# The attention's opening, and the gates of the second routing, of a macaron block rearranged

## Chip, cores and metric

One core of a Trainium2 chip runs the whole program. The metric is the device time of one execution in microseconds (us). A PE matmul's speed follows a clock that the profile gives as "granted clock", 1.00 being full speed.

## What is computed

An input x of 8 sequences x 1024 tokens x 512 features in f32, 8192 tokens in all, goes through three residual steps. The reference in short:

```python
x = x + 0.5 * moe(layernorm(x))
x = x + attention(layernorm(x))      # 16 heads of 32, rotary q and k, softmax(q k / sqrt(32)) v, then Wo
x = x + 0.5 * moe(layernorm(x))

def moe(h):                          # 32 experts, the same weights both times
    probs = softmax(h @ w_router)                    # one expert per token, the best
    top1 = argmax(probs); gate = probs[top1]
    pos = cumsum(onehot(top1)) - 1                   # the token's place in its expert, in order of tokens
    accepted = pos < 320                             # 1.25 * 8192 / 32
    y = (silu(buf @ w_gate) * (buf @ w_up)) @ w_down # buf: each expert's tokens
    return h + where(accepted, gate * y, 0)
```

## The kernel before

The program has six parts, one after the other. Times are those of the profiled execution.

- **First routing** (`front`, 0 to 114): all tokens are normalized and routed; it ends with the tables `come` (which token each of an expert's 3 blocks of up to 128 rows takes) and `go` (where its result goes).
- **First branch** (114 to 119): the program chooses one of four lists of expert widths by the counts. Each engine jumps by itself.
- **First experts** (`experts`, 119 to 877): for each of 32 experts POOL gathers rows by token, PE transposes, multiplies by the three weights, and POOL scatters the result. `fetch_gates` (L883) gathers each token's gate by token beside them; it runs only in this stage, from the tensor `gates`.
- **Attention** (`Attention`, 877 to 3571), in 32 units (sequence b, four heads c).
- **Second branch**, at 3571, and **second experts** (3575 to 4337), the same code with other sources.

Inside the attention PE, ACT, DVE and POOL do their instructions in the order in which the program records them; SP, which starts most transfers, has an order chosen by a scheduler.

*Opening* (L1569). The eight x tiles of the first sequence are fetched on SP in two halves of four; for each tile DVE takes the statistics (`measure`, L164 to L180), POOL the square root (L176), ACT normalizes (L185), PE transposes (L207), and ACT and DVE in turn copy into `hT` (L1619). On the second tile half k and q of the next positions can be made. `project` (L1661) makes q and k groups: eight matmuls (L1221), a bias, a turn for the rotary part (L1709) and its arithmetic, and copies of 32 rows into `swapped` and `cross` (L1732), which the scores read. The opening does k0 and q0 of the first 512 positions, then k1; q1 is left to the first stage.

*Stage* (`stage`, L1252). A stage has 16 slots and lays two things into each: the "top" scores of one unit (L1842, whose maximum DVE takes at L1850 and whose exponential and sum ACT takes at L1854; only the maximum and the sum are kept) and the weighted sums of the unit before (L1813, L1820, L1822, L1910). PE's free time in a slot is filled by `fill` (L1373): groups of q and k of the following unit, of values (`values`, L1753, 16 matmuls of L1240), or of the output. A group may lie in one slot or in pieces in several. The first stage has no unit before, so only top scores and groups: twelve whole groups in slots 0 to 11 and none in slots 12 to 15:

```python
v, self.v_groups = self.v_groups[:7], self.v_groups[7:]
return dict(zip((0, 2, 4, 6, 8), ahead + qk)) | dict(zip((1, 3, 5, 7, 9, 10, 11), v))
```

`joined` (L1466, begun in slot 0) multiplies the router into Wo (L1482) and afterwards the biases of v and o into rows (L1494, L1506). `prepare` (L1534) normalizes the next sequence during a stage.

*Second routing* (`finished`, L2048, `route`, L238). As soon as four tiles of the attention's output are done, their routing follows: maximum of the logits, place in the expert (a scan), the slot number, the square root of the variance (`scaled`), the exponentials and the gate. Then (L303) POOL scatters, for each of the four tiles, one pair (token, gate) a row into `table` (L307), 64 scatters in 16 routings. In the last routing the four scatters carry the token alone, ahead of the gate, and the gates go to a second table `late` by `Late.put` (L745) inside the second experts.

*Behind the second branch* (`places`, L765): SP reads the table (L778), DVE folds its last block, PE transposes it (L788), DVE makes `come` (L790) and `go`; after the first expert's up-projections the `late` table is read, added, and transposed as the gates.

## Time and profile before

| quantity | value |
|---|---|
| runs | 4362.11, 4370.67, 4372.54; median 4370.67 us |
| profiled execution | 4346.86 us, of it the span 4345.1 us |
| granted clock, mean | 0.987 |
| first unit's top scores to its last | 917.5 to 1003.0 us |
| units after it | about 78.6 us each |
| first gather of the second experts | 3577.11 us |
| scatters into the table | 60 land in 2.6 us, the late 4 in 6.6 us (medians) |

PE is TensorE's matmuls, PEld its weight loads, DVE VectorE, ACT ScalarE, POOL GpSimd, SP the engine that issues most transfers. In a line of instructions, the first number is the start in us, the second the duration; "x4" is a group of four; in brackets stands the idle time of the engine just ahead and what ended it. In a table of stretches, each engine has its busy time and number of instructions.

### The profile page before, as it was taken

To read this page: it belongs to the slowest core of one execution; us is meant where nothing else is said; L and a number is where in the kernel's file an instruction comes from. 1 tells how busy PE (TensorE), PEld (TensorE's weight loads), DVE (VectorE), ACT (ScalarE), POOL (GpSimd) and SP (SyncE) were. 2 spreads that over 40 slices of the span, in tenths; PEclk is the share of its full clock that TensorE was granted. 3 is DMA by queue.
4 is the path that set the end of the run, shared out by engine and by line. 5 is a ranking of instruction groups with operands and counts; after the bars stand their busy time and mean duration, and the time that the engine had idled before them with its cause. 6 is when DMAs were issued, how large, how long until landed. Compare 5 with 4: busy or idle time off the path is not lost.

```text
span 4345.1 us, 84352 instructions
## 1 busy us (share of the span) xinstructions
PE 4233.0 (97%) x32310; PEld 2407.5 (55%) x32310; DVE 2600.6 (60%) x4964; ACT 2616.9 (60%) x4325; POOL 1401.0 (32%) x1640
## 2 busy tenths in 40 slices
PE   8899999979999999999999999999999979999999
PEld 6566777844444444444444444444444436667777
DVE  8434433356766776876876776776866754344333
ACT  6112221237888888888888888888888842112121
POOL 7344444421222242242232232232232213333332
PEclk9999999989999999999999999999999989999999
DMA  4656666531112212212212212212212116566664
GB/s 157 217 185 204 206 204 229 197 111 48 50 42 71 79 46 65 80 48 65 77 48 65 79 47 65 81 47 63 80 42 60 38 59 206 191 202 202 217 228 162
DMA packets 310835, 495.59 MB, mean 114 GB/s; under 512 B 65049, under 2 KB 99235, under 8 KB 310418
## 3 DMA queue, kind: packets, MB, share of 16 engines
q1 hardware_dynamic: 269698, 412.06, 31.0%
q0 software_dynamic: 39776, 76.77, 5.5%
q8 instruction: 257, 4.21, 0.4%
q14 instruction: 160, 1.31, 0.1%
q10 hardware_dynamic: 944, 1.23, 0.1%
HBM read 379.85 MB, written 87.93 MB: 108 GB/s over the span
## 4 chain that ended last, share of the span: by engine, by line
PE 91%; DVE 3%; issue 2%; ACT 1%; POOL 1%; DMA 1%; POOLq 0%; ACTq 0%; SPq 0%; DVEq 0%
PE s L1240 11%; PE s L1842 11%; PE s L1221 11%; PE gp L969 10%; PE up L969 10%; PE s L1910 10%; PE s L1813 10%; PE yp L1015 9%; PE s L1806 4%; PE tp L957 2%; PE yp L1023 1%; DVE nm L1850 1%; ACT s L1854 1%; PE s L207 1%; DVE st L164 1%
## 5 line engine op out<-in xcount | busy, mean ns | idle before, releaser
L1850 DVE TENSOR_REDUCE nm<-s 128x1 f32<-128x1024 f32 x1024 | 1205.6, 1219 | 541.7 <-PE s L1842 540.3
L1854 ACT ACTIVATE s<-s,nm 128x1024 f32<-128x1024 f32 x1024 | 1114.3, 1088 | 149.9 <-DVE nm L1850 141.3
L974 ACT ACTIVATE sg<-gp 128x320 f32<-128x320 f32 (+7 forms) x256 | 99.5, 389 | 1061.8 <-PE gp L969 1060.8
L1820 ACT ACTIVATE pr<-s 128x512 f32<-128x512 f32 x992 | 538.1, 594 | 230.7 <-PE s L1813 226.8
L1748 POOL TENSOR_TENSOR raw<-raw,a 128x512 f32<-128x512 f32 x125 | 158.6, 1269 | 1312.6 <-DMA rot<-raw 957.3
L1842 PE MATMUL s<-cross,swapped 32*128 32x512 f32 x2048 | 560.4, 607 | 5.4 <-DMA cross<-k 3.1
L1842 PE MATMUL s<-k,q 32*128 32x512 f32 x2048 | 560.1, 603 | 0.0
L1822 ACT ACTIVATE pr<-s 128x1024 f32<-128x1024 f32 x528 | 542.9, 1031 | 19.7 <-PE s L1813 19.7
L1813 PE MATMUL s<-q,k 32*128 32x512 f32 x4096 | 538.4, 590 | 0.0
L1221 PE MATMUL s<-hT,wqk 128*32 128x128 f32 (+3 forms) x4720 | 503.3, 324 | 8.8 <-ACT pr L1820 4.9
L1910 PE MATMUL s<-pr,big 128*32 128x512 f32 x4096 | 492.7, 598 | 0.5 <-ACT pr L1822 0.5
L969 PE MATMUL gp<-bT,wg 128*128 128x272 f32 (+7 forms) x1984 | 488.7, 389 | 0.0
L969 PE MATMUL up<-bT,wu 128*128 128x272 f32 (+7 forms) x1984 | 484.9, 387 | 0.0
L1221 PEld LDWEIGHTS s<-hT,wqk 128*32 128x32 f32 (+1 forms) x4720 | 299.1, 129 | 286.1 <-ACT pr L1820 101.6
L1015 PE MATMUL yp<-wd,a 128*128 128x512 f32 x992 | 445.9, 592 | 0.0
L969 PEld LDWEIGHTS gp<-bT,wg 128*128 128x128 f32 x1984 | 371.6, 190 | 87.4 <-issue 21.4
L969 PEld LDWEIGHTS up<-bT,wu 128*128 128x128 f32 x1984 | 374.4, 190 | 70.3
L996 DVE TENSOR_TENSOR a<-sg,up 128x320 f32<-128x320 f32 (+7 forms) x256 | 110.6, 432 | 491.0 <-PE up L969 431.5
L1842 PEld LDWEIGHTS s<-k,q 32*128 32x128 f32 x2048 | 243.2, 183 | 102.0 <-DVE raw L1689 36.3
L1910 PEld LDWEIGHTS s<-pr,big 128*32 128x32 f32 x4096 | 106.7, 109 | 347.6 <-ACT pr L1820 187.4
L1019 DVE SCALAR_TENSOR_TENSOR ys<-yp,gates,x 128x512 f32<-128x512 f32 x128 | 96.1, 751 | 336.9 <-PE yp L1015 336.9
L1842 PEld LDWEIGHTS s<-cross,swapped 32*128 32x128 f32 x2048 | 224.4, 183 | 119.3 <-DVE raw L1689 22.8
(307 smaller groups left out, 5394.8 us busy)
## 6 DMA issues: line engine op xcount, KB each, us to landing
wg<-in_w_gate SPq DMA_DIRECT2D x62, 1024.0 KB
wu<-in_w_up SPq DMA_DIRECT2D x62, 1024.0 KB
wd<-in_w_down SPq DMA_DIRECT2D x62, 1024.0 KB
rot<-raw SPq DMA_DIRECT2D x1000, 32.0 KB
all<-in_x SPq DMA_DIRECT2D x32, 512.0 KB
xt<-first_rows SPq DMA_DIRECT2D x64, 256.0 KB
swapped<-q SPq DMA_DIRECT2D x256, 64.0 KB
xr<-first_rows SPq DMA_DIRECT2D x64, 256.0 KB
```

The lines of the kernel that those rows point to most:

```text
L969: nc.tensor.matmul(acc, w[:, k, f * P : (f + 1) * P], to.bT[:, k, 0:width], start=(k == 0), stop=(k == s.KD - 1),)
L1015: nc.tensor.matmul(yp, a[:, f, i * P : (i + 1) * P], wd[:, f, :], start=(f == 0), stop=(f == KF - 1),)
L1221: self.nc.tensor.matmul(acc[a : a + w, lo:hi], one[:, a : a + w], two[:, lo:hi], start=(i == 0), stop=(i == len(terms) - 1),)
L1240: self.nc.tensor.matmul(bank[a : a + w, 0 : to - at], one[:, a : a + w], two[:, at:to], start=(i == 0), stop=(i == len(terms) - 1),)
L1806: nc.tensor.matmul(sb[:, h, :], self.ones16[at : at + 3, :], row[at : at + 3, :], start=True, stop=False,)
L1813: nc.tensor.matmul(sb[:, h, :], k[at, t * P : (t + 1) * P], q[at, n * 512 : (n + 1) * 512], start=False, stop=True,)
L1820: nc.scalar.activation(pr[:, h, :], sb[:, h, :], AF.Exp)
L1822: nc.scalar.activation(pr, sb, AF.Exp)
L1842: nc.tensor.matmul(sa[:, m, :], (own if here else swapped)[at, at_q], ka[at, m * 512 : (m + 1) * 512] if here else cross[at, :], start=Tru ...
L1850: nc.vector.tensor_reduce(nm[:, j, h : h + 1], flat, AX.X, ALU.max, negate=True)
L1854: nc.scalar.activation(flat, flat, AF.Exp, bias=nm[:, j, h : h + 1], accum_out=se[pair][:, j, odd : odd + 1],)
L1910: nc.tensor.matmul(po[at : at + HD, :], self.v[b][t + j][:, c * P + at : c * P + at + HD], prs[h // 2 * 2][:, h % 2, :], start=(j == 0), s ...
```

## The change

The opening: the x tiles of the first half go ahead of the biases in SP's queue (`columns` is a function of its own, called later), the weights of v are loaded in the opening, the two operations that only other users of `normalizing` need (L179, L180) are left out here and in `prepare`, and tile 3 is normalized on DVE. After the second half's transposes come one group of values, k1, and another group of values. The values of the first sequence, except for the last tile, are copied on ACT. The first stage gets ten groups, of which four lie in a slot each and six in two.

Routing: the table has one column, the token. The scatters come after the square root and ahead of the gate; in the last routing ahead of the square root. The gate of each routing is written to a tensor by token: on SP, the last one on ACT. The second table and its clearing at the start (L2132), `places` and `Late` go. `placed` reads the table and makes `come` and `go` at the end of the attention, ahead of the branch. The second experts fetch their gates by token like the first.

With the SP order made by the scheduler, the built program's SP begins the attention so: cos, sin, x (4), wk, biases, wq, x (4), values' weights, wq, wo, woT. Before: cos, sin, biases, x (4), wq, wk, x (4), wq, values' weights, wo, woT.

```diff
@@ -176,8 +175,9 @@
...
         nc.vector.scalar_tensor_tensor(n, mv[:, :, 0], -1.0, r, ALU.mult, ALU.mult)
-        nc.vector.tensor_scalar(r2, r, 0.5, 1.0, ALU.mult, ALU.add)
-        nc.vector.tensor_scalar(n2, n, 0.5, None, ALU.mult)
+        if r2 is not None:
+            nc.vector.tensor_scalar(r2, r, 0.5, 1.0, ALU.mult, ALU.add)
+            nc.vector.tensor_scalar(n2, n, 0.5, None, ALU.mult)
         return r, n, r2, n2
@@ -295,25 +295,20 @@
...
 
-        def gate():
-            nc.vector.tensor_reduce(se, ex, AX.X, ALU.add)
-            nc.vector.reciprocal(se, se)
-            nc.vector.tensor_scalar(late.gate if late else row[:, :, 1], se, 0.5, None, ALU.mult)
-
         def put():
             for j in range(G):
-                if spaced and j:
+                if j and spaced:
                     yield WAIT, 1
...
                     out_offset=bass.IndirectOffsetOnAxis(ap=slot[:, j : j + 1], axis=0),
-                    in_=row[:, j, :],
+                    in_=self.token[:, t0 + j : t0 + j + 1],
                     in_offset=None,
...
         pos, s, u = narrow("pos"), narrow("s"), narrow("u")
-        slot = late.slot if late else narrow("slot", I32)
+        slot = narrow("slot", I32)
         nc.vector.tensor_reduce(pos, lg, AX.X, ALU.add)
@@ -330,20 +325,23 @@
...
         nc.vector.tensor_scalar(spare[:, tokens], u, float(self.T), None, ALU.add)
-        if late:
-            nc.vector.memset(row[:, :, 1], 0.0)
-            yield from put()
+        r = None if last else (yield from scaled())
+        yield from put()
         if ordered:
             at_once(ordered())
-        r = yield from scaled()
+        if last:
+            r = yield from scaled()
         yield DVE, 0.3
...
         yield DVE, 0.7
-        gate()
-        if not late:
-            yield from put()
+        nc.vector.tensor_reduce(se, ex, AX.X, ALU.add)
+        nc.vector.reciprocal(se, se)
+        nc.vector.tensor_scalar(gate, se, 0.5, None, ALU.mult)
+        if not last:
+            yield WAIT, 1
+        (nc.scalar if last else nc.sync).dma_start(store, gate)
 
@@ -698,23 +696,12 @@
...
                 expert = Expert(self, (wp, ap, ps), src, views, matrix, others)
-                if kept:
-                    expert.keep(kept)
-                else:
-                    places = expert.places(table, late)
-                    next(places)
-
-
+                expert.keep(kept)
                 now = expert.gather(0, widths[0])
...
                 following = expert.gather(1, widths[1])
-                then = None
-                if late:
-                    late.put(nc)
-                    next(places)
-                    then = lambda: next(places, None)
                 quarters = expert.quarters(widths)
@@ -761,42 +730,6 @@
...
         self.gates = self.ap.tile([P, self.s.NB * self.s.E], F32, tag="gates", bufs=1, name="gates")
-
-    def places(self, table, late):
-
-
...
-                more = ap.tile([R, P], F32, tag="more", bufs=1, name="more")
-                nc.sync.dma_start(more, late.table[0 : s.NS, :].rearrange("(r s) c -> r (s c)", s=P))
-                yield
-                nc.vector.tensor_tensor(rows[:, :, 1], rows[:, :, 1], more, ALU.add)
-                nc.vector.tensor_copy(rows[R - E : R, n:P, 1], rows[R - E : R, 0:n, 1])
...
@@ -986,8 +919,7 @@
...
         later = after and after()
-        if self.of is not None:
-            self.fetch_gates(now)
+        self.fetch_gates(now)
         for f in range(KF):
@@ -1348,6 +1280,27 @@
...
             rounds(1)
+
+    def placed(self):
+
+        nc, s, pool, E, n = self.nc, self.s, self.ranking, self.s.E, self.s.last
+        R = s.NB * E
+        rows = pool.tile([R, P], F32, name="rows")
+        come, go = (pool.tile([P, R], I32, name=name) for name in ("come", "go"))
+        self.kept = SimpleNamespace(rows=rows, come=come, go=go, gates=self.gates)
+        nc.sync.dma_start(
+            rows, self.whole_table[0 : s.NS, :].rearrange("(r s) c -> r (s c)", s=P)
+        )
+        nc.vector.tensor_copy(rows[R - E : R, n:P], rows[R - E : R, 0:n])
+        pt = self.take()[:, 0:R]
+        nc.tensor.matmul(pt, rows, self.ranks[0], start=True, stop=True)
+        nc.vector.tensor_scalar(come, pt, float(s.T - 1), None, ALU.min)
+        nc.vector.tensor_copy(go[:, 0 : R - E], pt[:, 0 : R - E])
+        for i in range(2):
+            p = slice(i * n, (i + 1) * n)
+            nc.vector.tensor_scalar(
+                go[p, R - E : R], pt[p, R - E : R], 2.0, float(i), ALU.mult, ALU.add
+            )
 
@@ -1374,9 +1327,18 @@
...
         if b == c == 0:
-            self.v_groups = self.values(0)
-            v, self.v_groups = self.v_groups[:7], self.v_groups[7:]
-            return dict(zip((0, 2, 4, 6, 8), ahead + qk)) | dict(zip((1, 3, 5, 7, 9, 10, 11), v))
+            v, self.v_groups = self.v_groups[:5], self.v_groups[5:]
+            work = [group for two in zip(ahead + qk, v) for group in two]
+            slots, at = {}, 0
+            for n, group in enumerate(work):
+                if n in (0, 2, 4, 6):
+                    slots[at] = (group, [(at, 0, 512)])
+                    at += 1
+                else:
+                    slots[at] = (group, [(at, 0, 256), (at + 1, 256, 512)])
+                    at += 2
+            assert at == self.SLOTS
+            return slots
         if b == 0:
@@ -1421,17 +1383,10 @@
...
         nc, s, KD, L = self.nc, self.s, self.KD, self.L
-        bq, bk, bv = self.biases[:3]
 
...
         self.bias = wp.tile([P, 3, KD], F32, name="bias")
-        for i, a in enumerate((bq, bk, bv)):
-            nc.sync.dma_start(self.bias[:, i, :], a)
-
         self.scale = 1.0 / math.sqrt(HD)
-        nc.vector.tensor_scalar(
-            self.bias[:, 0, :], self.bias[:, 0, :], self.scale, None, ALU.mult
-        )
 
@@ -1451,6 +1406,12 @@
...
         self.bo_cols = wp.tile([P, KD], F32, name="bo_cols")
+
+    def columns(self):
+
+        nc = self.nc
+        for i, a in enumerate(self.biases[:3]):
+            nc.sync.dma_start(self.bias[:, i, :], a)
         nc.sync.dma_start(self.bo_cols, self.biases[4])
@@ -1576,25 +1538,24 @@
...
                 t = half * 4 + j
-
                 tag, bufs = (("xt", 4), ("oT", 10))[half]
...
 
-        xs = [fetch(0)]
-        self.load_qk(0, 0, 0)
-        self.load_qk(1, 0, 0)
         nc.sync.dma_start(self.cs, self.cos)
         nc.sync.dma_start(self.sn, self.sin)
+        xs = [fetch(0)]
+        self.load_qk(1, 0, 0)
+        self.columns()
+        self.load_qk(0, 0, 0)
         xs.append(fetch(1))
+        self.load(2)
         bys, steps = [], []
...
             mv = pool.tile([P, 4, 2], F32, tag="mv", name="mv")
-            by = [
-                pool.tile([P, 4], F32, tag=name, name=name) for name in ("rstd", "nmr", "r2", "n2")
-            ]
+            by = [pool.tile([P, 4], F32, tag=name, name=name) for name in ("rstd", "nmr")]
             bys.append((mv, by))
@@ -1604,14 +1565,16 @@
...
             s.stats(pool, mv[:, j, :], xs[half][j])
-            steps.append(s.normalizing(pool, mv[:, at, :], [t[:, at] for t in by]))
+            steps.append(
+                s.normalizing(pool, mv[:, at, :], [*(t[:, at] for t in by), None, None])
+            )
             next(steps[-1])
...
 
-        def normalize(half, j):
+        def normalize(half, j, how=s.normalize):
             x = xs[half][j]
-            s.normalize(x, x, bys[half][1], j)
+            how(x, x, (*bys[half][1], None, None), j)
 
@@ -1623,12 +1586,15 @@
...
         at_once(steps[-1])
+        normalize(0, 3, s.normalize_)
         for j in range(4):
-            if j == 3:
-                normalize(0, j)
             turn(0, j)
         self.there.add((0, 0))
+        nc.vector.tensor_scalar(
+            self.bias[:, 0, :], self.bias[:, 0, :], self.scale, None, ALU.mult
+        )
         q0, k0, k1, q1 = self.project(0, 0, True)
+        self.v_groups = self.values(0)
         for j in range(4):
@@ -1643,9 +1609,10 @@
...
         self.there.add((0, 1))
+        self.whole(self.v_groups.pop(0))
         self.whole(k1)
-        self.load(2)
         self.finish()
+        self.whole(self.v_groups.pop(0))
         return [q1]
@@ -1756,7 +1723,7 @@
...
 
-            def group(t=t):
+            def group(t=t, late=b or t + 1 == LT):
                 at = self.v_next % 12
@@ -1770,7 +1737,7 @@
...
                     for to, of in parts:
-                        nc.vector.tensor_copy(v[:, to], of)
+                        (nc.vector.tensor_copy if late else nc.scalar.copy)(v[:, to], of)
                     if logits is not None:
@@ -2072,7 +2039,8 @@
...
             counted, scaled, lambda: self.carry,
-            late=self.late if last and half else None, spaced=not last,
+            self.gates[first * P : (first + 4) * P, :].rearrange("(t p) c -> p (t c)", p=P),
+            spaced=not last, last=last and half,
         )
@@ -2123,15 +2090,9 @@
...
     ):
-        none = pool.tile([P, s.NS // P, 2], F32, tag="none", bufs=1, name="none")
-        nc.gpsimd.memset(none[:, :, 0], float(T))
-        nc.gpsimd.memset(none[:, :, 1], 0.0)
-        nc.scalar.dma_start(table[0 : s.NS, :].rearrange("(p r) c -> p r c", p=P), none)
-        nothing = pool.tile([P, s.NS // P], F32, tag="nothing", bufs=1, name="nothing")
-        nc.gpsimd.memset(nothing, 0.0)
-        nc.scalar.dma_start(
-            late.table[0 : s.NS, :].rearrange("(p r) c -> p (r c)", p=P), nothing
-        )
+        none = pool.tile([P, s.NS // P], F32, tag="none", bufs=1, name="none")
+        nc.gpsimd.memset(none, float(T))
+        nc.scalar.dma_start(table[0 : s.NS, :].rearrange("(p r) c -> p (r c)", p=P), none)
         ranks = []
@@ -2157,13 +2118,11 @@
...
         ranking, (wqT, wkT, wvT, woT, wo), (bq, bk, bv, bo, boc), cos, sin,
-        late, big, weights,
+        gates[1], table, big, weights,
     )
...
 
-    s.experts(
-        table, attention.ranks, x2, of, weights, big, others=(*rest, spare), late=late
-    )
+    s.experts(attention.ranks, x2, of, weights, big, (*rest, spare), attention.kept)
 
```

## The prediction

> **What bounds the kernel now.** I read the page first, for the busy shares and the clock, then a table of busy times by stretch, for where the bound changes, and then the instructions of the changed stretches in order of time.
>
> ```profile
> span 4345.1 us, 84352 instructions
> ...
> PE 4233.0 (97%) x32310; PEld 2407.5 (55%) x32310; DVE 2600.6 (60%) x4964; ACT 2616.9 (60%) x4325; POOL 1401.0 (32%) x1640
> ...
> PE   8899999979999999999999999999999979999999
> ...
> PEclk9999999989999999999999999999999989999999
> ```
>
> PE is the bound, 97% busy; only around a fifth and four fifths of the span do its share and its clock dip. Those are the places that the change touches. The stretch table gives PE, PEld, DVE, ACT and POOL busy time, then the granted clock, the DMA share and GB/s:
>
> ```profile
> 876.00:918.00 42.00, 23.16 (x64) 11.27 (x64) 18.70 (x65) 11.47 (x16) 9.89 (x21) 0.76 0.63 204
> 918.00:995.00 77.00, 72.14 (x300) 39.65 (x299) 52.68 (x81) 31.51 (x54) 22.04 (x22) 0.94 0.20 51
> ...
> 1100.00:3440.00 2340.00, 2331.40 (x22876) 1123.11 (x22869) 1706.78 (x2695) 2023.69 (x3276) 659.06 (x775) 1.00 0.23 62
> 3540.00:3570.00 30.00, 18.03 (x90) 7.25 (x90) 22.90 (x85) 6.43 (x8) 9.85 (x10) 0.83 0.30 97
> 3570.00:3590.00 20.00, 5.23 (x17) 3.86 (x18) 7.09 (x29) 4.17 (x6) 6.80 (x10) 0.50 0.66 218
> ```
>
> The attention's 2340 us in the middle are PE without a gap at full clock: an operation saved there on another engine is worth nothing. PE is short of work in the attention's opening and first stage, and from its end to the second experts (3540 to 3590). The rest of the working is in those stretches.
>
> **Opening and first stage: the loss today.** The instructions in order of time (start, duration, in brackets the wait before):
>
> ```profile
> 885.69 0.69 DVE L164 BATCH_NORM_STATS2 st<-xt 128x6 f32<-128x512 f32 x1 [2.81 <-DMA xt<-first_rows]
> ...
> 892.91 0.81 ACT L185 ACTIVATE xt<-xt,nmr,rstd 128x512 f32<-128x512 f32 x1
> ...
> 895.75 9.57 PE L1221 MATMUL s<-hT,wqk 128*128 128x512 f32 x16 [0.85 <-DVE hT L1619]
> ...
> 911.98 3.70 PE L1221 MATMUL s<-hT,wqk 128*128 128x512 f32 x8 [3.02 <-DVE hT L1619]
> ...
> 921.72 1.19 PE L1842 MATMUL s<-cross,swapped 32*128 32x512 f32 x1 [3.09 <-DMA cross<-k]
> ```
>
> The reader sees two waits of 3 us with nothing to do, and 16 matmuls in 9.57 us, where a later 8 take 3.70. From 895.75 to the first filling group of the next stage at 1008.0 are 112.25 us. PE's work in it, at full-clock prices of rows of this trace: 8 q/k groups x 3.67, 7 v groups x 3.92, 17 slots of top scores x 1.07, 32 transposes 4.3, turns 3.1, joins 3.3, the rest 3.0: 88.7. So 23.5 us are lost: 10.7 idle (3.9 for hT, 3.1 for cross, 0.8 for raw, the rest for the exponentials L1854), 12.8 at a low clock. The first stage's last four slots hold no group and still take 15.6 us (987.4 to 1003.0), 3.9 each, since DVE's maxima (2 x 1.2) and ACT's exponentials (2 x 1.1) follow one another.
>
> **What the change does there.** (a) The x tiles are issued ahead of the three biases and the bias of o, which took SP from 880.92 to 882.83: 1.9 us. The two small DVE operations L179 and L180 (0.15 each, 0.19 of the tile's 1.26) go, and tile 3's normalization (ACT, 892.91, behind two copies) is done by DVE right after its statistics: 1.6. So k0 starts 3.5 us earlier, at 892.25. (b) One v group (3.9) goes ahead of k1, where PE waits 3.02, and one between k1's turn and the scores, where it waits 3.09; their copies are on ACT. They also keep the clock up where q1 now takes 5.51 instead of 3.70. (c) The first stage has ten groups instead of twelve, six of them in halves, so every slot has work. A half slot has 1.07 of scores and 1.85 to 1.95 of a group, and takes the 3.9 that the bare slots took, or 4.0: four whole slots at 4.95 (scores, group and transposes as in slots 0 to 11) and twelve at 4.0 are 67.8, against 85.5 (917.5 to 1003.0). The joins' bias products (4.4 us of PE at 1009.7 to 1017.7) fall in the half slots' gaps instead of the next stage.
>
> Loss left: 3 for the cold start of k0, 0.5 before the scores, 12 x 0.5 in half slots, 0.5 at the next stage: 10. Gain: 23.5 - 10 + 3.5 = **17**. Bounds: nothing left but the cold start gives 24; half slots wholly at half clock give 3 to 8 (first rival).
>
> **The routing on the way.** Each routing's four scatters now move after the square root and before the gate; a store of the gates by token (128x4, 512 elements) is added, 15 on SP and one on ACT. SP's queue holds, behind a store, loads of wq and the rot and swapped copies. PE's longest wait for such a copy in the whole trace is one, and POOL's are long without PE waiting after them:
>
> ```profile
> PE s L1842 <- DMA cross<-k: 3.1, 1, 3.1
> ```
>
> ```profile
> POOL raw L1748 <- DMA rot<-raw: 957.3, 93, 20.6
> ```
>
> I take 0. The trace has no such store. Bounds from the nearest rows: below, 0; above, the 2.6 us that one 128-element scatter needs to land, times four, 10.4 a store, all on the path. I choose 0 because copies in this queue are late by up to 20.6 us today without an idle PE in the steady stretch. The rule that speaks against it stands in the Trainium skill, "DMA: Bandwidth & Descriptors", Rules for kernel authors: a transfer whose last dimension isn't contiguous becomes one descriptor per element, and below 64 KB one pays mostly overhead. By it these are 512 descriptors for 2 KB; the page gives no time for that, and no row shows one.
>
> **End of the attention and the second branch.** Today POOL waits for the gate before the last-but-one scatters:
>
> ```profile
> 3556.11 1.06 POOL L307 DMA_INDIRECT table<-entries,slot  x1 [5.47 <-DVE entries L301]
> ...
> 3572.12 0.35 SPq L778 DMA_DIRECT2D slots<-table  x1
> ...
> 3577.11 1.03 POOL L875 DMA_INDIRECT x<-x,come  x1 [8.23 <-DMA all<-x]
> ```
>
> After, the scatters need the slots alone (3549.2), and go from 3550.7; the late four (slot at 3558.3) end at 3563.2 instead of 3566.0. They land 6.6 us after issue, or 2.6 as the other 60: 3564.8 to 3569. The table is read, folded, transposed and turned into addresses (5.0 us today from L778 to the gather) ahead of the branch: first gather at 3574.1 to 3576.8 instead of 3577.1. But DVE branches only behind the last address (`go`), so its statistics, at 3580.47 now, can be 0.8 later or 3.0 earlier: take **1.3**. If the read costs more than today, all of this is lost.
>
> **Second experts.** They read the gates by 82 more gathers on POOL, lose the addition of the late table and the 0.48 us matmul with its wait:
>
> ```profile
> 3607.99 0.48 PE L788 MATMUL pt<-matrix,slots 96*128 96x96 f32 x2 [1.07 <-DVE slots L786]
> ```
>
> The first experts already fetch so. Both stages in equal stretches:
>
> ```profile
> 200.00:876.30 676.30, 676.25 (x3078) 486.05 (x3076) 254.88 (x673) 137.55 (x247) 294.17 (x303) 1.00 0.61 202
> 3657.50:4333.80 676.30, 676.30 (x3083) 487.05 (x3083) 253.03 (x673) 137.50 (x248) 221.48 (x230) 1.00 0.61 201
> ```
>
> POOL's extra 73 us lie beside a PE that is full in both, so the gathers cost 0; without that cover they would cost 73. From the first gp to the last yp the second stage takes 747.4, the first 745.3: gain **2.1**, bounds 0 and 2.1.
>
> **Front.** One of two table clears and its ACT issue (1.14 us at 6.41, ahead of ACT's first work) goes: 0 to 1.1, take **0.6**.
>
> **Sum.** 17 + 1.3 + 2.1 + 0.6 = 21 off the profiled execution of 4346.86 (span 4345.1 and 1.8 around it): 4326. That execution is 23.8 below the median of the runs, 4370.67; the same 21 off the median is 4349.7, say **4350**.
>
> **Rivals.** (1) *The half slots lose the clock.* For it, PE's idle 1.77 us at 990.4 and the matmuls behind it:
>
> ```profile
> 992.21 0.69 PE L1842 MATMUL s<-cross,swapped 32*128 32x512 f32 x1 [1.77 <-ACT s L1854]
> ...
> 992.74 0.95 PE L1842 MATMUL s<-cross,swapped 32*128 32x512 f32 x1
> ```
>
> After it pieces are slower (0.95 and up to 1.22 for 0.59) until about 1000. Half slots idle 1 us each, in two parts. At half the clock a half slot is 2.14 + 3.8 = 5.9, twelve of them 71, the stage 71 + 20 = 91 instead of 68; but PE is then without a gap and should warm up again, so two thirds of this loss, 15 at the most, is my bound. Gain left in all 21 - 10 = 11 (6 to 13): 4360, within 0.3%. Against it: each gap is shorter than the one that did it. The Trainium skill, "TensorE: Matmul & The Clock Gate", Why this matters for your kernels, asks only for gaps under about 3 us, but its section on psum-queue depth-cycling says that frequent micro-idles between groups make the clock swing too. By the first the stage stays at 68, by the second it goes toward the rival; the 1.77 us row disagrees with the first.
>
> (2) *Slower: the gate stores hold up SP's queue.* SP waits, ahead of a new transfer, for one issued eight before; a store of 512 elements that lands late holds the rot, swapped and wq transfers behind it, and PE, in recorded order, waits at the next q/k group. The place is once per routing, 15 times. From 21 / 15 = 1.4 us each on PE's path the gain is gone, from 2.3 the kernel is slower by 0.3%; at 10.4 x 15 it would be +135. I price it at 2.4 us each, 36: 4350 + 36 = 4386. In the profile it would show as PE waits on rot or swapped in each unit with a routing, and a middle stretch with PE below 2331 of 2340. Against it: the slack of those copies above.
>
> (3) *The fill is hidden anyway.* The wvT and router loads, now between x and wo, may not have landed when v0 wants them (905.5), or DVE, 52.7 busy of 77 already, holds the slots at 4.5. Then 12 x 0.5 = 6 more, v0 gives 1 of its 3, the branch gives nothing: 21 - 6 - 2 - 1.3 = 11.7: 4359, within 0.3%.
>
> **How the numbers follow.** A measurement of this kernel tells about 0.3% (13 us) from no change: below 4357.6 is faster, above 4383.8 slower. Forecast (opening gains 10 or more, stores hidden) 0.66; rival 1 0.17; rival 3 0.10; rival 2 0.07. So faster 0.66, same 0.27, slower 0.07. The range: below, the forecast with the opening at 24, the branch at 3 and the front at 1.1 (30 in all: 4340) and 4 for the runs' own spread (10 between them); above, rivals 1 and 3 with the opening at 6 and the branch at -0.8 (gain 8: 4363) and 3 of spread. **4336 to 4366**; rival 2 is left out.
>
> **What would show it.** k0's first matmul about 11.7 us behind the landing of the first experts' last scatter (880.56 today, so 15.2). No wait over 1 us before k1 and the scores; the stage of the first tops 66 to 70 us between its first scores and the first L1806 (rival 1: a PEclk below 0.9 there; rival 3: waits on DVE or wvo); the middle stretch unchanged; the first gather of the second experts 1 to 3 us closer to the last scatter; first gp to last yp 745.3. Wrong: any new PE wait on DMA in the middle.

## The result, and the profile after

The changed kernel takes 4389.19 us (median of 5 runs, 4385.82 to 4394.58), before 4370.67 beside it (4362.11 to 4372.54): 1.0051 of before, 95% interval 1.0038 to 1.0064. Forecast was 4350. It is slower, by half a per cent, and the profile says that the opening did what was forecast all the same. The profiled execution is one of the five; its page:

```profile
span 4387.4 us, 84407 instructions
...
PE 4262.3 (97%) x32314; PEld 2418.0 (55%) x32314; DVE 2600.0 (59%) x4900; ACT 2620.9 (60%) x4338; POOL 1477.0 (34%) x1716
...
PE   8899999989999999999999999999999979999999
...
PEclk9999999999999999999999999999999989999999
```

PE's busy time grew by 29 us (4233.0 before) with the same work, so matmuls took longer somewhere. The page's tenths are too coarse for it; the table of stretches shows where (busy time of PE, PEld, DVE, ACT, POOL, then the granted clock):

```profile
915.00:991.00 76.00, 74.61 (x339) 39.63 (x340) 54.10 (x80) 41.59 (x76) 21.07 (x22) 1.00 0.22 57
1100.00:3440.00 2340.00, 2314.37 (x22422) 1110.77 (x22416) 1670.20 (x2599) 1976.50 (x3198) 642.66 (x759) 0.99 0.23 61
```

The first stage is full (clock 1.00, 0.94 before). The middle, which had 2331 of 2340 us busy and 22876 matmuls in that time, now has 2314 and 22422. To place the loss I noted for both traces when each unit's sums begin, and cut the span in three: opening up to the second unit's sums, the 30 units from there to the last, and the rest.

| part, us against the trace of before | forecast | changed kernel |
|---|---|---|
| opening and first two stages | -17 | -18.3 |
| the 30 units of the middle | 0 | +54.9 |
| end, branch, second experts | -3.4 | +5.8 |

In the middle nearly all of it comes in six units, one a sequence: 81.8 to 82.2 us each before, 88.3 to 90.1 after. (In the trace of before the 30 units of the middle take 76.9 to 82.2 us, 80.3 on average, more than the 78.6 given above.) They are those in which the two routings of the sequence before are done. The first of them, on PE; "issue" is idle time in which PE waited for nothing that the profile shows:

```profile
1534.39 0.37 PE L1773 MATMUL s<-mrow,ones 3*128 3x512 bf16 x1 [0.39 <-issue]
1535.13 0.37 PE L1773 MATMUL s<-mrow,ones 3*128 3x512 bf16 x1 [0.38 <-issue]
1535.86 0.38 PE L1773 MATMUL s<-mrow,ones 3*128 3x512 bf16 x1 [0.36 <-issue]
1537.28 1.11 PE L1780 MATMUL s<-q,k 32*128 32x512 f32 x3 [1.03 <-issue]
```

No DMA, no engine is waited for: instructions come one by one, for some 5 us, and then the clock is at half for 3.4 to 6.8 us. Meanwhile POOL does six of the routings' scatters in a row, with 0.3 us of idle time between them:

```profile
1530.01 1.00 POOL L302 DMA_INDIRECT table<-token,slot  x1 [0.16 <-issue]
...
1536.38 0.96 POOL L302 DMA_INDIRECT table<-token,slot  x1 [0.30 <-issue]
```

Before, the scatters of the one half had to wait for its gates, which kept them apart from those of the other; the same unit in the trace of before, where a row of three ends and the next scatter waits:

```profile
1552.88 0.96 POOL L307 DMA_INDIRECT table<-entries,slot  x1 [0.30 <-issue]
1558.22 0.96 POOL L307 DMA_INDIRECT table<-entries,slot  x1 [4.38 <-DVE entries L301]
```

The end, in order of time: POOL does the last scatter, ACT stores the last gates, SP reads the table, DVE folds it.

```profile
3598.55 0.95 POOL L302 DMA_INDIRECT table<-token,slot  x1 [0.30 <-issue]
...
3606.97 0.38 ACTq L344 DMA_DIRECT2D gates<-gate  x1
3609.90 0.33 SPq L1291 DMA_DIRECT2D rows<-table  x1
...
3620.51 0.19 DVE L1294 COPY rows<-rows 32x64 f32<-32x64 f32 x1 [13.57 <-DMA rows<-table]
```

The read is issued at 3609.9, 11.4 us behind the last scatter (before, 7.1), and used at 3620.5, 10.6 us later; before, 2.3 (3572.12 to 3574.45). Three microseconds ahead of it ACT had issued the last store of the gates.

### The profile page after: what moved, and what is told of

Read it like the earlier page. It is cut to its first block, busy times and chain, and to the rows that moved or that the text cites. A ratio compares the mean times of both kernels' runs of the same rounds, so it can differ in the third digit from the quotient of the medians.

```text
span 4387.4 us, 84407 instructions
## 1 busy us (share of the span) xinstructions
PE 4262.3 (97%) x32314; PEld 2418.0 (55%) x32314; DVE 2600.0 (59%) x4900; ACT 2620.9 (60%) x4338; POOL 1477.0 (34%) x1716
## 4 chain that ended last, share of the span: by engine, by line
PE 90%; DVE 3%; issue 2%; ACT 2%; DMA 1%; POOL 1%; SPq 0%; POOLq 0%; DVEq 0%; ACTq 0%
PE s L1171 11%; PE s L1809 11%; PE gp L902 10%; PE up L902 10%; PE s L1152 10%; PE s L1877 10%; PE s L1780 10%; PE yp L945 9%; PE s L1773 4%; PE tp L890 2%; PE yp L953 1%; ACT s L1821 1%; DVE nm L1817 1%; DMA table<-token,slot 1%; PE s L207 1%
## 5 line engine op out<-in xcount | busy, mean ns | idle before, releaser
L1787 ACT ACTIVATE pr<-s 128x512 f32<-128x512 f32 x992 | 538.6, 594 | 257.8 <-PE s L1780 248.9
L1809 PE MATMUL s<-cross,swapped 32*128 32x512 f32 x2048 | 577.3, 611 | 0.1
L1809 PE MATMUL s<-k,q 32*128 32x512 f32 x2048 | 573.2, 607 | 3.0 <-DVE raw L1656 2.3
L1780 PE MATMUL s<-q,k 32*128 32x512 f32 x4096 | 551.6, 595 | 3.6 <-issue 3.6
```

The lines of the kernel that those rows point to most:

```text
L1780: nc.tensor.matmul(sb[:, h, :], k[at, t * P : (t + 1) * P], q[at, n * 512 : (n + 1) * 512], start=False, stop=True,)
L1787: nc.scalar.activation(pr[:, h, :], sb[:, h, :], AF.Exp)
L1809: nc.tensor.matmul(sa[:, m, :], (own if here else swapped)[at, at_q], ka[at, m * 512 : (m + 1) * 512] if here else cross[at, :], start=Tru ...
```

## The experiments

Theory A: the scatters in a row slow PE. Theory B: the 4-byte stores do, in the middle and at the end. Eighteen kernels in five series were run; three further theories (C, D, E) came up on the way. The chips, or the places of the program on them, are of two kinds, told apart by before itself: **a**, where before takes 4353 us, and **b**, where it takes 4367 to 4371 (the first measurement was of that kind; the profile that the forecast used, 4346.86, was like a). Every ratio is to before in the same series. Six units: mean of the six with scatters. Parts in us against the trace of before; the opening's column holds some 3 us of spread from the program ahead of it. That trace is like kind a, so the rows of kind b also hold what kind b costs by itself.

| run | kind | us | ratio (95%) | opening | middle | end | six units |
|---|---|---|---|---|---|---|---|
| e1 opening only | a | 4333.0 | 0.9957 (0.9940 to 0.9974) | -17.7 | +0.6 | +0.3 | 81.8 |
| e2 scatters behind gate | a | 4338.8 | 0.9972 (0.9962 to 0.9982) | -15.5 | +3.5 | +3.6 | 82.2 |
| e3 one store | a | 4325.2 | 0.9937 (0.9920 to 0.9953) | -17.6 | +1.6 | -5.9 | 81.9 |
| e4 scatters spaced | a | 4343.0 | 0.9980 (0.9971 to 0.9990) | -18.5 | +7.5 | +4.9 | 81.7 |
| e5 changed kernel | a | 4352.3 | 0.9998 (0.9988 to 1.0007) | -15.7 | +17.2 | +3.3 | 83.5 |
| e6 stores on ACT | a | 4364.8 | 1.0030 (1.0019 to 1.0041) | -13.5 | +34.2 | +3.3 | 84.4 |
| e7 stores as rows | a | 4326.8 | 0.9936 (0.9920 to 0.9953) | -14.8 | +4.0 | -7.9 | 82.2 |
| e8 opening, extra stores | a | 4342.5 | 0.9972 (0.9961 to 0.9983) | -13.5 | +4.0 | +6.2 | 82.4 |
| e9 rows, extra 4 bytes | b | 4382.1 | 1.0033 (1.0020 to 1.0045) | -15.2 | +51.4 | -0.4 | 90.0 |
| e10 rows, extra 64 bytes | b | 4371.4 | 1.0011 (1.0001 to 1.0021) | -16.5 | +48.8 | -7.6 | 89.4 |
| e11 rows but at the end | b | 4381.3 | 1.0034 (1.0022 to 1.0047) | -15.8 | +48.0 | +3.3 | 89.4 |
| e12 opening, whole groups | b | 4353.7 | 0.9967 (0.9956 to 0.9978) | -11.5 | +14.1 | -0.1 | 83.5 |
| e13 one store | a | 4327.8 | 0.9947 (0.9931 to 0.9964) | -14.3 | +0.9 | -7.6 | 81.9 |
| e14 one store, scatters behind | a | 4322.3 | 0.9935 (0.9919 to 0.9952) | -16.9 | +0.3 | -8.1 | 81.9 |
| e15 one store, spaced | a | 4324.5 | 0.9937 (0.9920 to 0.9954) | -15.1 | +2.1 | -8.4 | 81.7 |
| e16 one store, 8 bytes | a | 4327.6 | 0.9945 (0.9929 to 0.9962) | -13.4 | +1.1 | -7.5 | 81.9 |
| e17 as e14 | b | 4350.3 | 0.9955 (0.9939 to 0.9972) | -11.6 | +30.3 | -7.9 | 86.4 |
| e18 as e16 | b | 4370.9 | 1.0011 (1.0001 to 1.0020) | -16.6 | +44.8 | -7.5 | 89.0 |

**The opening alone (e1, e12).** e1 is before with the opening's edits; e12 the same with ten whole groups in slots 0 to 9.

```diff
-                if n in (0, 2, 4, 6):
+                if n < 20:
                     slots[at] = (group, [(at, 0, 512)])
```

> Before with the new opening and first stage alone (x tiles ahead of the biases, two operations fewer, two value groups in the waits, ten groups of which six in halves); routing, table and branch as before. The trace of the changed kernel starts the second unit's sums 18.3 us earlier than before, and loses 7 to 8 us once in each of six sequences afterwards. If the loss comes from the routing (both theories below): 18 us faster than before, a middle without lost time. If the loss comes from the opening's edits (copies of values on ACT, another place of the weights): slower by 25 us or so, with the six losses in it.

> Before with the new opening alone, but the first stage's ten groups whole, in slots 0 to 9, and none in slots 10 to 15. By the prediction's sum the halves save what the bare slots lose: six bare slots at 3.9 against ten at 4.95 are 73 us, where twelve half slots gave 68 by forecast and 77 from the first scores to the sums by measurement (with the joins' products). So 5 to 10 us slower than the opening alone, 0.997 to 0.998 of before. If the gain comes only from the two value groups in the waits: within 2 us of it.

The opening's gain is the change's own, and nothing of the loss is: 17.7 us stay to the end. Without the halves 11.5 are left. Counted from the last yp of the first experts, which takes the spread out, the second unit's sums begin 213.3 us behind it in the kernel before, 195.9 in e1 and 202.3 in e12: of 17.4 us the halves are worth 6.5, and the two value groups with the earlier start the rest.

**One thing put back (e2, e3, e4), and the kernel again (e5).** e2 puts the scatters behind the gate again; e4 puts them three slots apart; e3 stores all gates once:

```diff
-        (nc.scalar if last else nc.sync).dma_start(store, gate)
...
+        gt = self.take()[0 : s.NT, 0:P]
+        nc.tensor.transpose(gt, s.gate, s.ident)
+        turned = pool.tile([s.NT, P], F32, name="turned")
+        nc.vector.tensor_copy(turned, gt)
+        nc.scalar.dma_start(self.gates.rearrange("(t p) c -> t (p c)", p=P), turned)
```

> The changed kernel with one thing put back: each routing's four scatters come behind the gate again (the last routing as it is); stores of the gates and everything else stay. Theory A (in six sequences the scatters of both halves now meet, six follow one another on POOL, and PE's instructions come slowly meanwhile): the scatters spread again, the six losses of 7 to 8 us go, about 45 us below the changed kernel. Theory B (the 4-byte stores of the gates hold up transfers and instruction loading): as the changed kernel, within 5 us.

> The changed kernel without its 16 stores of 512 elements: the gates of all tokens are kept and stored once at the end, turned by PE into 64 rows of 128. Theory A (six scatters in a row): the losses stay, as the changed kernel within 5 us, apart from 2 to 6 us at the end of the attention. Theory B (the stores): the six losses of 7 to 8 us go, about 45 us below the changed kernel.

> The changed kernel with its scatters three slots apart instead of one, so that they do not follow one another on POOL; gates stored as in the changed kernel. Theory A (six in a row): the losses go, about 45 us below the changed kernel. Theory B (the stores): they stay, within 5 us.

> The changed kernel once more, next to the others of this series, since the earlier four ran on a chip where before took 4353.6 us instead of 4370.7. If the six losses belong to the kernel: again 1.003 to 1.007 of before. If they belong to the chip of the first measurement: 0.995 to 1.0.

Set against the first measurement alone, each of e2, e3 and e4 would have looked like the cure; e5 shows that 37 us of the difference (4389.2 to 4352.3, the same kernel) go with the kind. On kind a the changed kernel is level with before, and taking out the stores gives 27 us (e5 to e3), 15.6 of them in the middle and 9.2 at the end: theory B. Theory A alone falls on kind a: e3 has the same six scatters in a row and loses nothing. But e2 and e4, which keep the stores and spread the scatters, also give 13.5 and 9.3.

**Queue or memory (e6, e7, e8).** e6 issues every store on ACT; e7 turns each routing's 128x4 gates into 4x128 before the store; e8 adds the stores to e1, unread.

```diff
+        gt = psum.tile([P, P], F32, tag=tag, name="gt")[0:G, :]
+        nc.tensor.transpose(gt, gate, self.ident)
+        nc.vector.tensor_copy(turned, gt)
+        (nc.scalar if last else nc.sync).dma_start(store, turned)
```

> The changed kernel with all 16 stores of the gates issued by ACT instead of SP. Theory C (order of SP's queue: the rot, swapped and weight transfers wait behind a store): the losses go, 35 to 45 us below the changed kernel. Theory D (512 elements of 4 bytes written to memory slow everything that reads or writes there, PE's instructions too): they stay, within 10 us.

> The changed kernel with each routing's gates turned by PE into 4 rows of 128 before the store, so that 16 stores of 4 x 512 bytes stand at the same places of the same queues. Theory C (order of the queue): the losses stay, within 10 us of the changed kernel. Theory D (512 small elements): they go, 35 to 45 us below it, about 0.994 to 0.996 of before; the turning costs 16 x 0.3 us of PE.

> Before with the new opening alone, and besides 16 stores of 512 elements of 4 bytes of the gates into memory that nobody reads, behind each routing's scatters; the table, its order and the branch as before. If the stores are enough by themselves (theory D): 25 to 45 us above the opening alone, 1.002 to 1.006 of before. If they cost only together with the scatters of one 4-byte element that stand close together (theory E): 0 to 8 us above the opening alone, 0.996 to 0.998 of before.

Theory C, the order of SP's queue, falls: as rows in the same queue the stores cost nothing (e7). On another queue they cost 12 us more (e6), but that test is less clean: in its middle PE waits 14.2 us for ACT's exponentials (L1787), 3.5 in e5, so the stores have a price of their own on ACT. The store's form is the cost, as theory D has it; what it holds up in the middle is not shown, and PE's instructions hardly are, with 1.7 us of "issue" there in e5. By itself (e8 against e1) the form costs only 9.5 us, 5.9 of them at the end. With the small stores the middle grows by 3.5 us where the scatters stay behind the gate (e2), by 7.5 where they are spaced (e4) and by 17.2 where they are in a row (e5), so there the stores need the scatters in a row to reach their full price (theory E). All of this is of kind a.

**Size of an element, and the end (e9, e10, e11).** Beside e7's stores, a second store from a table of constants that nobody reads, of 512 elements of 4 or of 64 bytes:

```diff
+            self.extra[t0 * P : (t0 + 4) * P, :].rearrange("(t p) c -> p t c", p=P),
+            self.ident[:, 0:64].rearrange("p (t c) -> p t c", c=16),
```

> The kernel with the gates stored as rows (4326.8 us, 0.9936 of before), and beside each of its 16 stores another of 512 elements of 4 bytes into memory that nobody reads, from a table of constants. If small stores are the cause by themselves, wherever the gates go: 18 to 30 us above it, 0.998 to 1.001 of before. If it was the wait for the gate: within 3 us of it.

> The same with 512 elements of 64 bytes a store, 64 bytes apart in memory, as many descriptors of another size. If the number of descriptors is the cost: as with 4 bytes, 18 to 30 us above the kernel with rows. If it is writing pieces of 4 bytes: within 6 us of the kernel with rows, 0.994 to 0.995 of before.

> The kernel with the gates stored as rows, but the last two stores (one on SP, one on ACT, both at the end of the attention) by elements of 4 bytes as in the changed kernel. From the end of the attention's sums to the end of the program the kernel with rows took 791.9 us, the changed kernel 803.1 to 805.6, before 799.8. If the loss at the end comes from these two stores: 10 to 13 us above the kernel with rows, 0.996 to 0.997 of before, with the table's read landing about 10 us after its issue. If it comes from the branch's new order: within 2 us of the kernel with rows.

This series fell on kind b, and there the six units lost 7 to 9 us in all three, stores as rows or not. My account of the loss by the stores alone fell with it. On the size of an element the series says less than it was meant to. The extra stores read constants, so nothing holds them back, and in SP's order, which the scheduler makes, 15 of the 16 run in the first routing, 43.8 to 80.6 us in e9 and here in e10:

```profile
L350 SPq DMA_DIRECT2D extra<-ident x15: 505/507/2622, 44.1 to 59.2; - x15
```

So their middles (51.4 and 48.8, against 48.0 in e11) tell nothing of the size. Only the last, on ACT, stands at the end of the attention, at 3608.5 and 3604.5, and there the two differ by 7.2 us: -0.4 with 512 elements of 4 bytes, -7.6 with 512 of 64 bytes, which is the end of the kernels without small stores. There the number of elements isn't the price, the piece of 4 bytes is. And with the last two stores alone by elements the end goes from -7.9 to +3.3 (e7, e11): the read is again issued 11.2 us behind the last scatter and lands 9.7 later, where e7 has 7.3 and 2.1.

**Scatters in a row (e13 to e18).** All four kernels have one store at the end, and differ in the scatters: as in the changed kernel; behind the gate; three slots apart; together, but with a table of two columns.

```diff
-    table = dram.tile([s.NS + T, 1], F32, name="table")
+    table = dram.tile([s.NS + T, 2], F32, name="table")
...
-                    in_=self.token[:, t0 + j : t0 + j + 1],
+                    in_=self.entries[:, t0 + j, :],
```

> The kernel with one store of the gates at the end, once more, beside three others that differ from it in the scatters alone. Where before takes 4353 us it took 4325 and lost nothing in the middle; where before takes 4368 us, no kernel without stores in the middle has run. If there the scatters alone cause the six losses: 4365 to 4375 us, 1.000 to 1.002 of a before of 4368. If stores were needed too: 0.994.

> The same with the scatters behind the gate, so that they lie as before in groups of at most three or four, elements of 4 bytes. If six in a row decide: the losses of 7 to 9 us a sequence fall to 0 to 2.5, 4330 to 4345 us where before takes 4368. If the element of 4 bytes decides: they stay, within 5 us of the kernel that it differs from.

> The same with the early scatters three slots apart. If six in a row decide: as with the scatters behind the gate, 4330 to 4345 us where before takes 4368. If the element of 4 bytes decides: within 5 us of the kernel that it differs from.

> The same with a table of two columns that both hold the token, so that a scatter writes 8 bytes an element as before; six still follow one another. If six in a row decide: within 5 us of the kernel that it differs from. If the element of 4 bytes decides: the losses go, 35 to 45 us below it where before takes 4368. The table's read moves twice the bytes, up to 1 us.

> The kernel with one store and the scatters behind the gate, again, for a chip on which before takes 4368 us. There, if six in a row decide: the units with scatters take 82 to 84.5 us as in before, 4330 to 4345 us. If the element of 4 bytes decides: 89 us, 4365 to 4375 us. On a chip where before takes 4353 us: 4322 again, and the question stays open.

> The kernel with one store, early scatters and a table of two columns, again, for a chip on which before takes 4368 us. There, if six in a row decide, whatever the element and without any store: the units with scatters take 88 to 91 us, 4365 to 4375 us. If the element of 4 bytes or the stores decide: 82 to 84.5 us, 4330 to 4345 us. On a chip where before takes 4353 us: 4327 again.

The first four fell on kind a and told nothing apart there, 4322 to 4328 us. The last two fell on kind b, where e18 has no store in the middle and 8 bytes an element, and its six units still take 87.8 to 90.2 us: the loss needs neither small element nor store. e17, whose longest row is four, takes 86.4, less than e18 by 2.6 a unit but more than I expected (82 to 84.5), so it fits neither reading set down for it; e12, with before's rows of three at most, takes 83.5. The same 100 us, first e13 (a), then e18 (b), both with six scatters in a row:

```profile
1500.00:1600.00 100.00, 99.13 (x977) 47.67 (x977) 75.14 (x131) 86.62 (x142) 42.35 (x48) 1.00 0.21 44
```

```profile
1500.00:1600.00 100.00, 96.79 (x898) 45.27 (x894) 69.59 (x123) 79.91 (x131) 36.89 (x40) 0.97 0.18 40
```

PE executes 79 matmuls fewer in e18; on PE stand the same waits as in the changed kernel, here e18's:

```profile
1535.70 0.37 PE L1780 MATMUL s<-mrow,ones 3*128 3x512 bf16 x1 [0.32 <-issue]
...
1538.57 1.12 PE L1787 MATMUL s<-q,k 32*128 32x512 f32 x3 [1.04 <-issue]
```

The traces tie these waits to the rows. Idle time of PE that "issue" ended comes to 14.7 to 16.4 us in the middle (1100 to 3440) of the five traces of kind b with rows of six (the changed kernel, e9, e10, e11, e18), all of it between a row's first scatter and 8 us behind its last. It is 0 in e17 and 0.2 in e12, also of kind b; on kind a it is 0 in every trace but e5's (1.7, away from the rows). That it is the length of the row, and not the scatters' earlier place, is argued and not shown: spaced early scatters (e15) ran on kind a alone.

Why PE gets its instructions slowly then, and why only on kind b, stays open. One sign: the transfers' issues with their median time to landing, of e13 and then of the changed kernel, whose trace has no landing of these scatters:

```profile
table<-token,slot POOLq DMA_INDIRECT x64, 2.4
```

```profile
table<-token,slot POOLq DMA_INDIRECT x64
```

All traces of kind b lack them, all of kind a have some (8 of 64 in e5, 48 in e3). A scatter that stands alone leaves 16 landing events in the packed trace, so a row of six should leave 96: e18 and the changed kernel have 9 to 25 of them, e13 has 87 to 96. On kind b a row of four (e17) leaves 33 to 44 of 64, one of three (e12) 28 to 35 of 48. So records are lost on kind b, most of them where PE is slow, and the recording of events itself may be part of the slow issue; a run without records wasn't tried.

**The best version** tried is e14 (and e17): one store of turned gates, scatters behind the gate, all else as changed. It is 0.9935 of before on kind a and 0.9955 (0.9939 to 0.9972) on kind b. On kind a e3, e7 and e15 (0.9936 to 0.9937) are not told apart from it, on kind b neither is e12 (0.9967, 0.9956 to 0.9978).

## Why the prediction was wrong

- **Opening and first stage, -17: right.** Measured -18.3, -17.7 alone, and counted from the last yp of the first experts 17.6 and 17.4. k0 starts at 891.45, 4.3 us earlier than before (forecast 3.5), with no wait above 1 us before k1 and the scores. In its parts the sum was less exact, and that the total came out is partly luck: the scores begin at 914.84, 2.7 us earlier than before, since cross is there by the time the second value group is done; the first stage takes 76.8 us, not 67.8, because its half slots take 4.5 each and its whole ones 5.8 (forecast 4.0 and 4.95), several of both with the joins' products; the next stage is 7.0 shorter, the joins' products (4.4 in the forecast) being gone from it. The first rival (half slots at half clock) is out: granted clock 1.00.

```profile
891.45 7.13 PE L1152 MATMUL s<-hT,wqk 128*128 128x512 f32 x16 [0.85 <-DVE hT L1582]
...
905.74 3.60 PE L1152 MATMUL s<-hT,wqk 128*128 128x512 f32 x8
...
911.08 3.83 PE L1171 MATMUL s<-wvo,hT 128*128 128x272 f32 x16
```

- **"Each routing's four scatters now move after the square root and before the gate": no price was given to the move.** This step failed most. The wait for the gate had also kept the scatters of a sequence's two halves apart. On kind b, against before's scatters on the same chip, the row of six costs 5.9 us a unit (89.4 in e11, 83.5 in e12), and 33.9 of the middle: 48.0 in e11, where no store of 4 bytes is left there, against 14.1 in e12. (Those 14.1 may be part of the 23.8 by which before's median lies above its trace; no trace of before on kind b was kept.)
- **The 15 stores, "I take 0": failed.** On kind a they cost 15.6 us in the middle and 9.2 at the end (e5 against e3), on kind b 6.9 in the middle (the changed kernel, 54.9, against e11). The bounds held (0 to 10.4 each), the choice didn't: I reasoned from the slack of SP's queue, and it isn't SP's queue (e7). The second rival had the sign and the place, with a chance of 0.07, but not the mechanism, transfers held behind the store: PE has no wait on rot or swapped in the changed kernel's middle, and as rows in the same queue the stores cost nothing. The Trainium skill, "DMA: Bandwidth & Descriptors", Rules for kernel authors, did speak against such a store; at the end of the attention e10 shows as many elements of 64 bytes for nothing, so there the rule's count is not what costs, the 4-byte piece is. For the middle no run parts the two.
- **The branch, 1.3, "if the read costs more than today, all of this is lost": that condition came true.** The read was issued some 4 us late and took 10.6 us behind the store of the gates. (How landings at 3564.8 to 3569 and 5.0 us more become a first gather at 3574.1 to 3576.8, the forecast does not work out.) Without small stores the read takes 2.1 and the whole end gains 7.9 (e7), more than the 3.4 forecast for branch and experts: first gp 3.9 us sooner after the last sums, the experts 1.8 shorter (745.6 from the first gp to the last yp; forecast 745.3), and 2.2 behind the last yp, where I hadn't looked.

```profile
3558.76 0.32 SPq L1296 DMA_DIRECT2D rows<-table  x1
3560.89 0.18 DVE L1299 COPY rows<-rows 32x64 f32<-32x64 f32 x1
```

- **Second experts: right**, 82 more gathers without a cost: from the first gp to the last yp 746.3 us (before 747.4, forecast 745.3). The front's 0.6 is below what these traces tell apart.
- **The base.** The trace that I took durations from is like kind a and the median of kind b. I noted the 23.8 us between them and carried the difference over unchanged. From the sum's 4326 to the profiled 4389.2 are 63 us: 54.9 in the middle, 9.2 at the end, 1.3 less in the opening. On kind a the same change gives 0.9998, on b 1.0051.

## What to carry to other kernels

A wait that looks like a delay also spaces what stands behind it: before moving an issue ahead, list what it will then stand next to on its engine. A store in pieces of 4 bytes was priced here by what ran beside and right after it, not by its queue; turning it on PE first saved 25 us (e7 against e5, kind a) and cost at most 3.4 (middle of e7 against e1). When an experiment adds an instruction, look in its trace for where it ran: 15 of 16 stores of e9 and e10 had moved out of the stretch that they were to test. And where the profiled execution and the median differ by more than the change's gain, the difference needs an explanation before a sum made on the one is moved to the other.

## What the hardware showed that I had not expected

- Six scatters of 128 elements in a row on POOL slow PE's instructions on kind b (87.8 to 90.2 us a unit in e18) and on kind a not at all (81.7 to 82.2 in e13).
- On kind b PE's clock also fell where rows of four are left and no wait on "issue" stands. In e17 PE stood still once in each of the six units, 1.48 us in the first and 0.8 in the others, and then ran at half clock for 3.4 us, in all six; the 8 us around the first pause and the 8 us after:

```profile
1543.97 0.83 PE L1812 MATMUL s<-k,q 32*128 32x512 f32 x1 [1.48 <-DVE raw L1659]
```

```profile
1536.00:1544.00 8.00, 6.52 (x77) 2.76 (x72) 3.41 (x7) 4.34 (x7) 5.77 (x6) 1.00 0.28 51
1544.00:1552.00 8.00, 8.00 (x42) 3.28 (x46) 4.28 (x10) 5.79 (x11) 0.00 (x0) 0.79 0.17 38
```

The Trainium skill, "TensorE: Matmul & The Clock Gate", What's actually happening, gives a free-running window of about 3.4 us for such changes; the length agrees. The pause alone does not decide: the same kernel on kind a (e14) pauses 0.8 us once in each of these sequences without a fall. In e17 PE had also been slow just ahead of the pause (eight matmuls of L1783 in 1.84 us, 1.03 in e14).
